# Graph attention in two layers: strip 0 of the next graph placed inside the previous graph's last sum

## Chip, cores and metric

One core of a Trainium2 chip. The core has five engines with an instruction queue each: TensorE (PE; its weight loads are a row of their own, PEld), VectorE (DVE), ScalarE (ACT), GpSimd (POOL) and SyncE (SP, which here issues most DMAs). The metric is the device time of one execution in microseconds; less is better. All times of the document are microseconds (us) unless they say ns.

## What is computed

16 graphs of 1024 nodes with 256 features, and a symmetric 0/1 adjacency with ones on its diagonal. Each graph passes through two attention layers, with a residual and a layer norm after each. The inputs give layer 0 one kind of edge only (`adj == 1`), so the reference comes down to this:

```
# layer 0, for one graph: x is 1024 x 256
e     = leaky_relu((x * a0) @ x.T, 0.2)
alpha = where(adj == 1, sigmoid(e), 0)
x     = layernorm(x + alpha @ x + bias)
# layer 1
H  = x @ W
s  = H @ a[:256];  d = H @ a[256:]
w  = where(adj != 0, exp(-leaky_relu(s[:, None] + d[None, :], 0.2)), 0)
h  = (w @ H) / w.sum(-1)
x  = layernorm(x + elu(h))
```

## The kernel before

The nodes of a graph are cut into 8 tiles of 128. For layer 0 the kernel computes only the upper triangle of the scores: strip `jt` holds rows of tile `jt` against the columns of tiles `jt` to 7. The lower triangle is the mirror image of it.

A strip goes through four steps, all written out by hand in program order (the schedule is manual; each engine takes its own instructions in that order, and waits on semaphores where it needs another engine's or a DMA's result):

- `strip` (L240): PE multiplies (L254) into one or two PSUM tiles of the pool `ps_e`, which has three. ACT takes Tanh twice, into `tb` (L262) and `low` (L263), and DVE takes the maximum (L264).
- `finish` (L270): DVE multiplies the strip with the adjacency into the tile `al`, which has one buffer.
- `dump` (L290, L294): DVE transposes `tb` in 32 x 32 blocks, and SP writes it to DRAM in four DMAs, so that DRAM holds the strip's mirror image `mir`. `tb` has four buffers.
- `gather` (L298): SP fetches the mirror image back, one DMA, into the column of `al` below the diagonal; `mask` (L305) then multiplies it with the adjacency on DVE. `add_twice` (L284) adds 2 on the diagonal, on POOL.

SP issues its DMAs in program order, and each of them uses one of eight semaphores in turn, so that a DMA can also have to wait for an earlier one's landing.

The loop over graphs `b` is a pipeline over three of them. An iteration does layer 0 of graph `b`, layer 1 of graph `prev = b - 1` and the output of graph `done = b - 2`:

- The strips of `b` (loop over `jt`, L783). After strip `jt` the list `projects` names the tiles of layer 1 of `prev` that are projected there: `project` (L582) multiplies `yT` with `W` into a PSUM tile of the pool `ps_acc`, which has three. ACT takes three small exponentials and scalings of it (L592 to L594) and evicts it as `H` (L603). The eviction of one projection is issued with the next projection. Also in this loop: dumps, gathers (`gather(b, jt - 1)` after dump `jt`, so fetch 0 stands behind dump 1), the deviations of the last two tiles of `done` (L344, ACT), and, from `jt` 4 on, the masks and the sums of blocks of `al` (`combine_al`, L455) that the seven products need.
- The seven block products of `alpha @ x` (L477: tiles `pQ`, `pV`, `pW`, `pR`), in Strassen's manner, evicted to `yT` and written to DRAM in row order (`turn_y`) and read back as rows `x1` (`fetch_y`). Product 1 (`pQ`) and product 5 (`pV`) stand between strips 4 and 7. `weights` (L637) makes layer 1's weights of `prev` on DVE.
- The sum of layer 1 of `prev` (L642), tile by tile. Tiles 0 to 2 run side by side, tiles 3 to 7 one after the other. The loop over `t` (L903) also holds the work behind each tile's sum: `elu` (DVE inverts the row sum, L678 and L679; ACT takes Relu and Exp, L687 and L688), `add` (DVE, L693 and L695), `deviation1` of the tile before and `deviation0` of graph `b` (ACT, L344), `roots0` on POOL, which gives the scalings `rcol` that the projections of `b` need, and `combine_x` for `b + 1`.

The adjacency of `b + 1` is loaded in two halves by POOL: rows of tiles 0 to 3 once `fetch_y` has landed (L888), rows of tiles 4 to 7 at tile 5 of the sum (L923). The PSUM pools of the sum's tiles are given by the string "aaeettat": tiles 2 and 3 take from `ps_e`, tiles 0, 1 and 6 from `ps_acc`, tiles 4, 5 and 7 from `ps_t`.

Of the kernel before, what the change touches and what calls it, by code (L numbers as in the profile page):

```python
# [30 lines left out]
def one_kind_pass(  # L31
# [35 lines left out]
    NT = N // P  # L67
# [172 lines left out]
    def strip(b, jt):  # L240


        if jt == 0:
            als[b] = one.tile([P, NT, N], F32, tag="al", name=f"al_{b}")
        width = N - jt * P
        tb = four.tile([P, N], F32, tag="tb", name=f"tb_{b}_{jt}")
        tbs[b, jt] = tb
        n_chunks = -(-width // HALF)
        per = -(-(width // P) // n_chunks) * P
        for n, o in enumerate(range(0, width, per)):  # L250
            w = min(per, width - o)
            pe = ps_e.tile([P, HALF], F32, tag="e", name=f"pe_{b}_{jt}_{n}")
            for c in range(ND):
                nc.tensor.matmul(  # L254
                    pe[:, 0:w],
                    lhsT=xTs[b][:, c, ts(jt, P)],
                    rhs=xas[b][:, c, ds(jt * P + o, w)],
                    start=(c == 0),
                    stop=(c == ND - 1),
                )  # L260
            low = two.tile([P, HALF], F32, tag="low", name=f"low_{b}_{jt}_{n}")
            nc.scalar.activation(tb[:, ds(o, w)], pe[:, 0:w], AF.Tanh, scale=0.5)  # L262
            nc.scalar.activation(low[:, 0:w], pe[:, 0:w], AF.Tanh, scale=0.5 * SLOPE)  # L263
            nc.vector.tensor_tensor(tb[:, ds(o, w)], tb[:, ds(o, w)], low[:, 0:w], ALU.max)  # L264
# [31 lines left out]
    def gather(b, t):  # L296

        nc.sync.dma_start(  # L298
            als[b][:, t + 1 :, ts(t, P)], mirs[b, t].rearrange("(jt p) i -> p jt i", p=P)
        )  # L300
# [406 lines left out]
    def deviation1(b, t):  # L707
        deviation(ys[b][t], mv1s[b][:, t, :])
# [66 lines left out]
    for b in range(1, B):  # L775
        prev, done = b - 1, b - 2
        last = b == B - 1

        projects = [[0, 1], [2], [3], [4, 5], [6, 7], [], [], []]
        if prev == 0:  # L780

            projects = [[], [], [0, 1], [2, 3], [4, 5, 6, 7], [], [], []]
        for jt in range(NT):  # L783
            if jt == 4:
                mask(b, 0, 0, HT)
                combine_al(b, 1, 0, 2)
            if jt == 5:
                new_yT(b)
                product(b, 1)
                mask(b, 1, 0, HT)  # L790
                save_p(prev, 0, NT, nc.scalar)
                share_p(prev, 0, NT)
                combine_al(b, 1, 2, 3)
                mask(b, 0, HT)
                mask(b, 1, HT)
                mask(b, 2, 0, HT)
                combine_al(b, 1, 3, HT)
                mask(b, 2, HT)
                if done >= 0:
                    r1s[done] = center(mv1s[done], f"1_{done}", unit=1.0 / D)  # L800
            if jt == 6:
                unite(b, "p1")
                product(b, 5)
                unite(b, "p5")
                combine_al(b, 2, 0, HT)
            strip(b, jt)
            if jt == 5:
                mask(b, 3, HT)
            finish(b, jt, ends=False)
            if jt == 4:  # L810
                gather(b, 3)
            if jt < NT - 1:
                dump(b, jt)
            if jt < 2 and done >= 0:
                deviation1(done, NT - 2 + jt)
            if prev == 0 and jt == 0:
                turn_x1(0, 0)
            if prev == 0 and jt == 1:
                transpose_x1(0)
            if jt >= 1 and jt != 4:  # L820
                gather(b, jt - 1)
            if jt < 4 and b == 1:
                combine_x(b, jt)
            for t in projects[jt]:
                project(prev, t)
            if jt == 4:
                evict_H()
            add_twice(b, jt)
        if not last:
            new_xT(b + 1)  # L830
            load_blocks(xTs[b + 1], x[b + 1], 0, N)

        def extras(n):
            if prev == 0 and n < 2:
                scale0(0, HT + 2 * n)
                scale0(0, HT + 2 * n + 1)
            elif prev > 0:
                scale0(prev, 2 * n)
                scale0(prev, 2 * n + 1)
            if done >= 0:  # L840
                for q in (2 * n, 2 * n + 1):
                    scale1(done, q)
                    if q == 3:
                        store(done, 0, HT)
            if n < 3:
                check_adj(b, n)

        product(b, 3)
        combine_al(b, 3, 0, HT)
        extras(0)  # L850
        product(b, 6)
        weights(prev, 0)
        mask(b, 4)
        mask(b, 5)
        combine_al(b, 4, 0, 2)
        mask(b, 6)
        combine_al(b, 4, 2, HT)
        unite(b, "u2")
        extras(1)
        product(b, 7)  # L860
        extras(2)
        product(b, 2)
        extras(3)
        unite(b, "s")
        unite(b, "c12")
        unite(b, "c22")
        unite(b, "c11")
        product(b, 4)
        turn_y(b, 0)
        if done >= 0:  # L870
            store(done, HT, HT)
        weights(prev, 1)
        weights(prev, 2)
        weights(prev, 3)
        weights(prev, 4)
        unite(b, "c21")
        turn_y(b, 1)
        fetch_y(b, 0)
        fetch_y(b, 1)
        if not last:  # L880
            load_x(b + 1, [nc.sync])
        check_adj(b, 3)
        weights(prev, 5)
        weights(prev, 6)
        weights(prev, 7)
        check_pq(prev)
        if not last:
            load_adj(b + 1, 0, behind=x1s[b][:, HT, 0:1])  # L888

        def sum_of(t):  # L890
            homes = {"a": (ps_acc, "acc"), "e": (ps_e, "e"), "t": (ps_t, "t")}
            return acc1(prev, t, *homes[("aaeteeaa" if last else "aaeettat")[t]])

        n_first = 3
        first = [sum_of(t) for t in range(n_first)]
        for m in range(NT):
            for t in range(n_first):
                sum1(prev, t, first[t], m)
        if not last:
            turn_x(b + 1, 0, False)  # L900
            turn_x(b + 1, 1, False)
        rinvs = invert_sums(prev, first)
        for t in range(NT):  # L903
            if t >= n_first:
                acc = sum_of(t)
                for m in range(NT):
                    sum1(prev, t, acc, m)
            if last and t == 7:
                for m in range(4):
                    weights(b, m, 0, HT)  # L910
            elu(prev, t, *((first[t], rinvs[t]) if t < n_first else (acc,)))
            if last and t in (2, 3):
                for q in range(HT):
                    stats0(b, (t - 2) * HT + q)
                roots0(b, t - 2)
            if t >= 1:
                add(prev, t - 1)
            if t >= 2:
                deviation1(prev, t - 2)
            if not last and t in (3, 5):  # L920
                sums0(b, (t - 3) // 2)
                if t == 5:
                    load_adj(b + 1, 1, behind=mv0s[b][:, HT, 0:1])  # L923
            if not last and t >= 4:
                for q in range(2 * t - 8, 2 * t - 6):
                    deviation0(b, q)
                if t % 2 == 1:
                    roots0(b, (t - 5) // 2)
            for n in ([0], [1], [2, 3])[t - 5] if not last and t >= 5 else []:
                combine_x(b + 1, n)  # L930
            if t == 3 and not last:
                scale_x(b + 1, 0)
                scale_x(b + 1, 1)
            if last and t in (4, 6):
                t0 = (t - 4) // 2 * HT
                for n in range(HT):
                    project(b, t0 + n)
                evict_H()
                save_p(b, t0, HT, nc.gpsimd)
                share_p(b, t0, HT)  # L940
            if last and t in (5, 7):
                for q in range(HT):
                    scale0(b, (t - 5) // 2 * HT + q)
            if last and t == 7:
                for m in range(4, 6):
                    weights(b, m, 0, HT)
        if not last:
            add(prev, NT - 1)
# [522 lines left out]
```

## Time and profile before

| what | value |
|---|---|
| median of 3 runs | 1219.75 us |
| lowest, highest | 1218.95, 1220.93 us |
| the profiled execution | 1221.67 us |
| its span, first to last instruction | 1219.9 us |
| granted TensorE clock in it | 0.998 |
| busy: PE matmul | 1208.1 us (99%), 4385 passes |
| busy: PE weight load | 820.6 us (67%) |
| busy: DVE | 993.7 us (81%) |
| busy: ACT | 842.8 us (69%) |
| busy: POOL | 385.5 us (32%) |
| SP's DMA queue | 136.90 MB, 56.5% of 16 engines' span |
| POOL's DMA queue | 41.95 MB, 18.6% |

A float32 matmul runs as two passes, each with its own weight load, so a count of passes is twice that of instructions. In a row of the timeline, the numbers are the start and the time taken, in us; then the engine, the line of the code, the operation, output and input by name, the sizes and how many were merged; in square brackets, how long the engine stood idle before it and what ended that. "SPq" rows are DMA issues. A row of the table by stretches gives a stretch, its length, the busy time of PE, PEld, DVE, ACT and POOL with the number of instructions, the granted clock, the mean busy share of the 16 DMA engines and the GB/s that they moved. A busy share says how long an engine had an instruction at work; whether another could have begun sooner is read from the starts.

### The profile page before, as it was taken

Reading aid. Unit: us, or ns where it says so; the run is one execution under the profiler, and the core shown is the slowest. Engines: PE = TensorE matmul, PEld = TensorE weight load, DVE = VectorE, ACT = ScalarE, POOL = GpSimd, SP = SyncE. Lnnn points to the kernel's source line nnn. Section 1 sums busy time; section 2 is a strip of 40 time slices with the busy share of each in tenths; the row PEclk is TensorE's granted clock in tenths of the full one; section 3 lists DMA queues with packets and bytes.
Section 4 is the critical chain, followed back from the end, with each engine's and each line's share of the span. In section 5 each row is a group of like instructions: output and inputs, shape, how many; then the busy total and the mean of one; then the engine's idle time right before and its main releaser. Section 6 shows DMA issues by size and latency. Waiting matters only on the chain.

```text
span 1219.9 us, 15900 instructions
## 1 busy us (share of the span) xinstructions
PE 1208.1 (99%) x4385; PEld 820.6 (67%) x4385; DVE 993.7 (81%) x1774; ACT 842.8 (69%) x2135; POOL 385.5 (32%) x715
## 2 busy tenths in 40 slices
PE   9999999999999999999999999999999999999997
PEld 7766758576575766758667485675857657576686
DVE  5698797887979879797897978979788896887966
ACT  3574866678677676876768766786676867667674
POOL 2220332414334043431424324143340433303343
PEclk9999999999999999999999999999999999999999
DMA  9568787697877968788787986978769787797412
GB/s 194 104 131 149 122 151 173 132 182 137 155 155 152 193 124 152 155 153 182 148 154 142 164 180 132 169 143 151 170 138 189 130 156 153 152 188 135 108 52 72
DMA packets 605080, 180.66 MB, mean 148 GB/s; under 512 B 482612, under 2 KB 587448, under 8 KB 604984
## 3 DMA queue, kind: packets, MB, share of 16 engines
q1 hardware_dynamic: 582800, 136.90, 56.5%
q0 software_dynamic: 20528, 41.95, 18.6%
q10 hardware_dynamic: 1656, 0.72, 0.2%
q8 instruction: 37, 0.61, 0.2%
q14 instruction: 59, 0.48, 0.1%
HBM read 152.44 MB, written 60.62 MB: 175 GB/s over the span
## 4 chain that ended last, share of the span: by engine, by line
PE 95%; DMA 2%; DVE 1%; ACT 1%; SPq 0%; issue 0%; ACTq 0%; DVEq 0%
PE acc L642 36%; PE pe L254 19%; PE pW L477 8%; PE pH L582 8%; PE pV L477 8%; PE pQ L477 8%; PE pR L477 4%; PE acc L396 2%; DMA al<-mir 1%; SPq L294 0%; DMA mir<-tb 0%; DMA x<-in_x 0%; PE pal L313 0%; PE pxT L230 0%; DVE al L270 0%
## 5 line engine op out<-in xcount | busy, mean ns | idle before, releaser
L642 PE MATMUL acc<-H,e 128*128 128x257 f32 x2032 | 444.8, 380 | 0.0
L642 PEld LDWEIGHTS acc<-H,e 128*128 128x128 f32 x2032 | 384.8, 190 | 63.4 <-issue 7.2
L254 PE MATMUL pe<-xa,xT 128*128 128x384 f32 (+1 forms) x720 | 250.0, 487 | 0.0
L254 PEld LDWEIGHTS pe<-xa,xT 128*128 128x128 f32 x720 | 134.4, 190 | 91.7 <-issue 52.9
L284 POOL TENSOR_TENSOR al<-ident,al 128x128 f32<-128x128 f32 x128 | 111.5, 879 | 201.7 <-DVE al L270 201.6
L637 DVE SCALAR_TENSOR_TENSOR e<-p,pq_kept,adj 128x1024 f32<-128x1024 f32 (+1 forms) x136 | 159.9, 1229 | 0.2 <-DMA p<-p_row 0.2
L262 ACT ACTIVATE tb<-pe 128x512 f32<-128x512 f32 (+1 forms) x192 | 93.8, 489 | 90.8 <-PE pe L254 63.9
L455 DVE TENSOR_TENSOR al<-al 128x1024 f32<-128x1024 f32 (+2 forms) x105 | 143.7, 1369 | 5.1
L264 DVE TENSOR_TENSOR tb<-tb,low 128x512 f32<-128x512 f32 (+1 forms) x192 | 104.2, 548 | 41.1 <-ACT low L263 41.0
L130 ACT ACTIVATE junk<-adj,minus 128x2048 bf16<-128x2048 bf16 x64 | 127.4, 1990 | 0.0
L582 PE MATMUL pH<-Wx,yT 128*128 128x258 f32 x480 | 116.4, 380 | 0.0
L104 POOL CAST adj<-x 128x1 bf16<-128x1 f32 x15 | 2.8, 187 | 348.7 <-DMA x<-y_rows 273.8
L582 PEld LDWEIGHTS pH<-Wx,yT 128*128 128x128 f32 x480 | 91.2, 190 | 31.1 <-issue 13.4
L477 PE MATMUL pV<-al,S 128*128 128x512 f32 x240 | 109.4, 595 | 0.9 <-DVE al L455 0.9
L305 DVE SCALAR_TENSOR_TENSOR al<-al,adj 128x512 f32<-128x512 f32 (+3 forms) x150 | 83.1, 570 | 30.9 <-DMA al<-mir 30.9
L477 PE MATMUL pW<-al,x 128*128 128x512 f32 x240 | 107.9, 592 | 0.0
L477 PE MATMUL pQ<-al,x 128*128 128x512 f32 x240 | 107.9, 592 | 0.0
L270 DVE SCALAR_TENSOR_TENSOR al<-tb,adj 128x512 f32<-128x512 f32 (+7 forms) x132 | 97.4, 738 | 4.5
L263 ACT ACTIVATE low<-pe 128x512 f32<-128x512 f32 (+1 forms) x192 | 94.0, 489 | 1.2 <-DVE tb L264 1.2
L668 ACT ACTIVATE sums<-acc,tiny 128x1 f32<-128x1 f32 x45 | 11.8, 262 | 118.2 <-PE acc L642 118.2
L379 ACT ACTIVATE y_kept<-y_kept,mr,r 128x256 f32<-128x256 f32 x120 | 64.9, 589 | 34.3 <-POOL mr L374 33.2
L477 PEld LDWEIGHTS pW<-al,x 128*128 128x128 f32 x240 | 45.5, 190 | 57.5 <-issue 55.3
(147 smaller groups left out, 1631.9 us busy)
## 6 DMA issues: line engine op xcount, KB each, us to landing
adj<-in_adjT POOLq DMA_DIRECT2D x30, 1024.0 KB, 8.3
x<-in_x SPq DMA_DIRECT2D x15, 1024.0 KB
y_rows<-Z SPq DMA_DIRECT2D x240, 64.0 KB
x<-y_rows SPq DMA_DIRECT2D x30, 512.0 KB
out<-y_kept SPq DMA_DIRECT2D x30, 512.0 KB
xT<-in_x SPq DMA_DIRECT2D x112, 128.0 KB
p<-p_row POOLq DMA_DIRECT2D x15, 512.0 KB, 4.1
mir<-tb SPq DMA_DIRECT2D x60, 112.0 KB
```

What stands on the lines that cost most here:

```text
L130: nc.scalar.activation(junk, rows, AF.Square, bias=minus1, scale=2.0, accum_out=chk[:, b * CHECKS + n : b * CHECKS + n + 1],)
L254: nc.tensor.matmul(pe[:, 0:w], lhsT=xTs[b][:, c, ts(jt, P)], rhs=xas[b][:, c, ds(jt * P + o, w)], start=(c == 0), stop=(c == ND - 1),)
L262: nc.scalar.activation(tb[:, ds(o, w)], pe[:, 0:w], AF.Tanh, scale=0.5)
L263: nc.scalar.activation(low[:, 0:w], pe[:, 0:w], AF.Tanh, scale=0.5 * SLOPE)
L264: nc.vector.tensor_tensor(tb[:, ds(o, w)], tb[:, ds(o, w)], low[:, 0:w], ALU.max)
L270: nc.vector.scalar_tensor_tensor(als[b][:, jt, c0:c1], tbs[b, jt][:, c0 - jt * P : c1 - jt * P], 1.0, adjs[b, jt // HT][:, jt % HT, c0:c1] ...
L284: nc.gpsimd.tensor_tensor(diag, ident2, diag, ALU.add)
L455: nc.vector.tensor_tensor(out_, in0, in1, ALU.subtract)
L477: nc.tensor.matmul(banks[bank], lhsT=lhs[:, jt, :], rhs=rhs[:, jt, :], start=first and jt == 0, stop=jt == HT - 1, skip_group_check=True,)
L582: nc.tensor.matmul(pt, lhsT=x1Ts[b][:, c, ts(t, P)], rhs=Wx[:, c, :], start=(c == 0), stop=(c == ND - 1),)
L637: nc.vector.scalar_tensor_tensor(e, p_bcs[b][:, cols], q, rows, ALU.mult, ALU.min)
L642: nc.tensor.matmul(acc, lhsT=es[b][:, m, ts(t, P)], rhs=Hs[b][m], start=(m == 0), stop=(m == NT - 1),)
```

## The change

Three edits, for graphs 2 to 15 (graph 1 keeps its order):

- Strip 0 of graph `b + 1` with its product with the adjacency and its dump is issued in the sum of layer 1 of `prev`, ahead of tile 6. So that tile 5's `add` and tile 4's `deviation1` do not stand behind it, they are moved up in front of it.
- In the next iteration the loop over strips leaves those steps out at `jt` 0 and issues the fetch of mirror 0 there, ahead of strip 1 and dump 1 instead of behind dump 1.
- The projections stand behind strips 1, 2, 3 and 4, two to a strip, where they stood behind strips 0 to 4 as 2, 1, 1, 2, 2.

```diff
-        projects = [[0, 1], [2], [3], [4, 5], [6, 7], [], [], []]
+        projects = [[], [0, 1], [2, 3], [4, 5], [6, 7], [], [], []]
...
-            strip(b, jt)
+            ahead = jt == 0 and b > 1
+            if not ahead:
+                strip(b, jt)
             if jt == 5:
                 mask(b, 3, HT)
-            finish(b, jt, ends=False)
+            if not ahead:
+                finish(b, jt, ends=False)
             if jt == 4:
                 gather(b, 3)
-            if jt < NT - 1:
+            if jt < NT - 1 and not ahead:
                 dump(b, jt)
...
+            if ahead:
+                gather(b, 0)
-            if jt >= 1 and jt != 4:
+            if jt >= (1 if b == 1 else 2) and jt != 4:
                 gather(b, jt - 1)
...
         for t in range(NT):
+            if t == 6 and not last:
+                add(prev, t - 1)
+                deviation1(prev, t - 2)
+                strip(b + 1, 0)
+                finish(b + 1, 0, ends=False)
+                dump(b + 1, 0)
             if t >= n_first:
                 acc = sum_of(t)
...
-            if t >= 1:
+            if t >= 1 and (last or t != 6):
                 add(prev, t - 1)
-            if t >= 2:
+            if t >= 2 and (last or t != 6):
                 deviation1(prev, t - 2)
```

The instructions are the same in kind and number on every engine; only their order changes.

## The prediction, made before the changed kernel had run

> **What bounds the kernel now.** The page first: TensorE (PE) is busy for nearly the whole span and makes up nearly the whole chain that ended last.
>
> ```profile
> PE   9999999999999999999999999999999999999997
> ...
> PE 95%; DMA 2%; DVE 1%; ACT 1%; SPq 0%; issue 0%; ACTq 0%; DVEq 0%
> ```
>
> As the ends of matmuls are modelled, I took their starts. Successive matmul passes begin 0.216 us apart at 257 columns, 0.322 at 384 and 0.429 at 512, in every stage and every graph. All passes at these spacings add up to 1197.6 us; from the first to the last start there are 11.9 us more. 9.2 of these lie in the start-up, in graph 1 (one wait for an evicted accumulator, 0.8 us) and in the last graphs' tail, which the change leaves alone. The other 2.7 us are seven gaps. Six of them are one place, the product V of a graph, which waits for `combine_al`, which waits for a mirrored strip. Graph 2, timeline of PE, DVE and SP:
>
> ```profile
> 154.65 1.02 PE L477 MATMUL pQ<-al,x 128*128 128x512 f32 x2
> 156.80 2.74 PE L477 MATMUL pV<-al,S 128*128 128x512 f32 x6
> 160.05 1.12 PE L477 MATMUL pV<-al,S 128*128 128x512 f32 x2 [0.51 <-DVE al L455]
> ```
>
> ```profile
> 158.90 0.29 DVE L305 SCALAR_TENSOR_TENSOR al<-al,adj 128x128 f32<-128x128 f32 x1 [1.25 <-DMA al<-mir]
> 159.30 0.69 DVE L455 TENSOR_TENSOR al<-al 128x512 f32<-128x512 f32 x1
> ```
>
> ```profile
> 140.62 5.73 SPq L294 DMA_DIRECT2D mir<-tb  x8
> 146.52 0.45 SPq L298 DMA_DIRECT2D al<-mir  x1
> 147.41 3.03 SPq L294 DMA_DIRECT2D mir<-tb  x4
> 150.55 0.45 SPq L298 DMA_DIRECT2D al<-mir  x1
> 151.04 4.49 SPq L294 DMA_DIRECT2D mir<-tb  x4
> 155.69 1.75 SPq L298 DMA_DIRECT2D al<-mir  x2
> ```
>
> Six passes from 156.80 make the seventh due at 156.80 + 6 x 0.429 = 159.37; it begins at 160.05, 0.68 late, and the pair lasts 1.12 where the pair of product Q lasts 1.02: 0.78 us in all. DVE waited 1.25 us for the fetch of mirror 2. On SP's queue that fetch is the first of the last row. The gaps at V: 0.78, 0.68, 0.28, 0.20, 0.23, 0.27 us (graphs 2, 3, 4, 10, 11, 15), sum 2.44; the seventh, 0.26, is a late weight of layer 1 in graph 3. So 2.7 us is what any change here can win.
>
> **The change, part by part.** Times below are counted from the first matmul of tile 5 of layer 1's sum (272.10 us in the span for graph 4), where both orders still agree.
>
> PE: the same matmuls in another order, and the third projection (`pH` of tile 3) is due at 22.08 in both, in all 14 graphs. Cost 0 while no operand is late.
>
> Mirrors. In graph 4 dump 0 is issued at 18.8, fetch 0 at 25.0, dump 2 at 25.6, fetch 1 at 29.4. Dump 2 stands behind fetch 0, which lands at 29.6: its four issues take 3.6 us and its first part lands at 30.1, where dump 1, with no fetch ahead of it, takes 2.1 to 2.6 us in the graphs. Fetch 1 follows dump 2, lands at 33.2; the last part of dump 3 waits for that landing (they share a semaphore), and fetch 2 stands behind it, at 33.6. After the change fetch 0 goes out when dump 0 has landed, about 17.2 (below), and lands about 21.4, ahead of dump 1 at 22.4. Dump 2 begins 0.2 later (below), 25.8, is issued in dump 1's 2.1, so fetch 1 goes out at 28.1, 1.3 earlier. It lands 1.7 behind the last landing of dump 2 (as before), 30.0 + 1.7 = 31.7, 1.5 earlier, and fetch 2 with it. The largest gap at V is 0.78: all six close, with 0.6 us or more to spare, and DVE reaches the weights earlier too, so the seventh closes. Gain 2.7; bounds 0 (rival B) and 2.7.
>
> ACT and DVE, the price of it. Rows of graph 4 around strip 0:
>
> ```profile
> 287.11 0.60 ACT L263 ACTIVATE low<-pe 128x512 f32<-128x512 f32 x1
> 287.59 0.52 ACT L344 ACTIVATE dev_junk<-y_kept,mv 128x256 bf16<-128x256 f32 x1
> ...
> 288.08 0.28 ACT L592 ACTIVATE H<-pH,rcol 128x1 f32<-128x1 f32 x1
> ...
> 289.37 0.46 ACT L603 ACTIVATE H<-pH,wr 128x256 f32<-128x256 f32 x1
> ```
>
> ```profile
> 287.75 0.69 DVE L264 TENSOR_TENSOR tb<-tb,low 128x512 f32<-128x512 f32 x1 [0.28 <-ACT low L263]
> 288.53 1.23 DVE L270 SCALAR_TENSOR_TENSOR al<-tb,adj 128x1024 f32<-128x1024 f32 x1
> 289.79 1.11 DVE L290 STREAM_TRANSPOSE tb<-tb 128x896 f32<-128x896 f32 x1
> ```
>
> I walk the new order with the spacings of these rows. ACT ends tile 5's two deviations as before, then deviation of tile 4 at 6.76 and the four Tanh at 7.26, 7.74, 8.22, 8.69. DVE: second maximum 0.64 behind the last Tanh, 9.33; product with the adjacency 0.78 later, 10.11; transpose 1.26 later, 11.37; only behind it (1.03) the inverse sum of tile 6, 12.41. ACT's `elu(6)` waits for that: 12.86, after 3.7 us with nothing to do. From there ACT never waits: two evictions 0.37 + 0.36, deviations 0.63 + 0.51, `elu(7)` 0.37 + 0.36, four deviations 0.63 x 3 + 0.51, four Tanh of strip 1 0.48 + 0.48 + 0.39 + 0.37, a deviation 0.49, then the projections' seven small ones 1.28: the eviction of the first projection (L603) begins at 21.34 and ends at 21.80. PE needs it for `pH` 3, the fourth project in a ring of three accumulators, at 22.08: 0.28 ahead.
>
> What a shorter lead costs: three places of the trace show it. Where the releaser ended 0.094 us after the matmul was due, PE lost 0.150 + 0.106; 0.521 after, 0.577 + 0.104; 0.039 before (graph 1's `pH`), 0.015 + 0.105. So the loss is 0.16 minus the lead. With 0.28 it is 0, and 0.12 is left over; the links' spread in the 14 graphs is 0.01 to 0.02 each. Between 0 and 0.16 x 14 = 2.2 us (lead gone) I take 0. ACT is then 0.5 behind the old order at strip 2, whose transpose ends 0.2 later (25.81 for 25.61); at projects 4 to 7 it has caught up.
>
> The adjacency. Strip 0's finish now comes at 10.1 instead of 16.4, and needs the half of the next adjacency whose load is issued about -1. It lands at 6.6 to 9.0 in 13 graphs and at 10.5 in graph 7. Cost there 0.4 - 0.12 = 0.3 us; elsewhere 1.1 us or more of cover. If all loads were as late, 14 x 0.3 = 4 us; I take 0.3.
>
> DMA. The mean share of the DMA engines in stretches of 3 us, graph 4:
>
> ```profile
> 284.00:287.00 3.00, 3.00 (x10) 1.69 (x10) 2.08 (x6) 2.93 (x10) 1.62 (x3) 1.00 0.87 165
> 287.00:290.00 3.00, 3.00 (x11) 1.74 (x10) 2.60 (x4) 2.94 (x12) 2.59 (x6) 1.00 0.00 0
> ...
> 299.00:302.00 3.00, 3.00 (x12) 1.87 (x11) 1.32 (x3) 2.54 (x9) 0.46 (x1) 1.00 1.01 212
> ```
>
> Dump 0's four writes and fetch 0 leave the full stretch at 299 (1.01) for 284.6 to 293, of which 3 us stood empty. They meet the tail of the other adjacency half (lands 15.1, needed at 31): if both ran at half speed there, dump 0 lands 2.5 later and fetch 0 at 24, needed at 28.6. No cost. On SP nothing stands behind dump 0 and fetch 0 until dump 1; the fetch's wait for dump 0's landing (4.6 us after issue) ends at 17.2. POOL's second set of `roots0` starts 3.7 us later with deviation (17.4) and ends about 22.4; project 4 needs it at 26.6. Cost 0.
>
> Sum: 1221.67 us for the profiled execution (span 1219.9 and 1.8 around it) - 2.7 + 0.3 = 1219.3. That execution is 1.9 above the median of the runs, 1219.75. If the 1.9 is all late mirrors, the median run has 0.8 of them to lose: 1219.3. If none of it is: 1217.4. I take the middle, **1218.4**, own range 1217.2 to 1219.6.
>
> [...]
>
> **Rivals.**
> A, slower: ACT's walk is later than I make it, at `elu(6)` behind DVE's finish and transpose, and `pH` 3 waits in every graph. For it: ACT is busy 2.9 of 3 us there (the 284 and 287 rows), and only 0.12 us is to spare. Against: every link is a row. It decides from 0.12 us; the gain of 1.35 in the median is used up at 0.12 + 1.35/14 = 0.22 us. At 0.4: 1218.4 + 14 x 0.28 = 1222.3.
> B: dump 2's slow issues are not fetch 0's doing. Then its 0.2 us later start makes each of the six gaps 0.2 larger and opens some 0.15 in two graphs with little lead: 1219.75 + 1.5 + 0.3 = 1221.5.
> C, faster beyond the measure: the profiled execution's extra time is fixed, and the runs have all 2.7 us of gaps or more: 1217.0.
> D: PE has room that starts don't show. The idle of the strips' weight loads is 57.0 us in 238 waits, 0.24 each; strip 0's four in 14 graphs would give 13.4: 1206.
>
> **How the numbers follow.** Forecast 0.44, A 0.25, B 0.14, C 0.14, D 0.02, none of these 0.01. What a measurement of this kernel tells from no change is about 0.2%, 2.4 us: faster is below 1217.3 (C, D and a little of the forecast), slower above 1222.2 (most of A, a little of B). Faster 0.17, within 0.58, slower 0.25. Range 1216.9 to 1222.6, which leaves out D and the late end of A.
>
> **What would show it.** V's last pair 1.02 us long in all graphs, and DVE's L305 no longer idle for mirror 2; fetch 0 issued near 17 and dump 2's four issues in 2.1 us; ACT idle 3.7 us ahead of `elu(6)`; `pH` 3 at 22.08. Wrong: a gap of PE at `pH` 3 in every graph (A), gaps at V still there (B), DVE waiting at L270 for `adj` in more than one or two graphs.

## The result and the profile after

The changed kernel's median is 1216.93 us (1215.74 to 1218.59, 13 runs); the kernel before, run beside it, has 1219.75 (1218.89 to 1222.18, 13 runs). The ratio is 0.9975, 95% interval 0.9967 to 0.9984: 2.8 us faster, where 1.35 was forecast. The profiled execution took 1216.93, with a span of 1215.1 and a granted clock of 0.998.

The page of after, busy shares of PE in 40 slices and the chain of work that ended last:

```profile
PE   9999999999999999999999999999999999999997
...
PE 90%; DVE 3%; DMA 2%; ACT 2%; issue 1%; SPq 1%; POOL 0%; ACTq 0%; DVEq 0%; POOLq 0%
```

PE is as full as before. The chain has 3% of DVE and 2% of ACT, because it is followed back through one place where PE did wait (graph 11's `pH`, below).

Product V of graph 2, timeline of PE and of DVE:

```profile
154.51 3.60 PE L477 MATMUL pV<-al,S 128*128 128x512 f32 x8
157.95 1.25 PE L254 MATMUL pe<-xa,xT 128*128 128x256 f32 x6
```

```profile
155.11 0.29 DVE L305 SCALAR_TENSOR_TENSOR al<-al,adj 128x128 f32<-128x128 f32 x1 [0.99 <-DMA al<-mir]
155.50 0.69 DVE L455 TENSOR_TENSOR al<-al 128x512 f32<-128x512 f32 x1
```

The eight passes are one row now: from 154.51 to 157.95 they take 3.44 = 8 x 0.43, with no gap. DVE still waits for mirror 2, 0.99 us, but its `combine_al` ends at 156.19, and the seventh pass is due at 154.51 + 6 x 0.429 = 157.08. A wait is there, and it costs nothing. SP's queue in the same graph:

```profile
132.01 2.85 SPq L294 DMA_DIRECT2D mir<-tb  x4
137.35 0.38 SPq L298 DMA_DIRECT2D al<-mir  x1
141.88 5.62 SPq L294 DMA_DIRECT2D mir<-tb  x8
147.66 0.41 SPq L298 DMA_DIRECT2D al<-mir  x1
148.14 3.54 SPq L294 DMA_DIRECT2D mir<-tb  x4
151.85 1.74 SPq L298 DMA_DIRECT2D al<-mir  x2
```

Fetch 0 (137.35) is alone between dump 0 and dump 1; the next row is dumps 1 and 2 in one, and fetch 1 follows at 147.66. Over all graphs DVE waited for mirrors 30.9 us before and 11.7 after, by the list of waits (total, times, longest), first of before, then of after:

```profile
DVE al L305 <- DMA al<-mir: 30.9, 31, 1.6
```

```profile
DVE al L305 <- DMA al<-mir: 11.7, 15, 1.4
```

Strip 0 in graph 4, DVE and then ACT. From tile 5's first matmul (268.10 here) the product with the adjacency begins at 10.12, `elu(6)` at 12.83, and the eviction of the first projection ends at 21.74:

```profile
278.22 1.23 DVE L270 SCALAR_TENSOR_TENSOR al<-tb,adj 128x1024 f32<-128x1024 f32 x1
279.48 1.11 DVE L290 STREAM_TRANSPOSE tb<-tb 128x896 f32<-128x896 f32 x1
```

```profile
280.93 0.47 ACT L687 ACTIVATE h<-acc,rinv 128x256 f32<-128x256 f32 x1 [3.52 <-DVE rinv L679]
...
289.38 0.46 ACT L603 ACTIVATE H<-pH,wr 128x256 f32<-128x256 f32 x1
```

What is new on PE's path is `pH` of tile 3 in a few graphs. Graph 11, PE, DVE and ACT:

```profile
810.00 1.03 PE L582 MATMUL pH<-Wx,yT 128*128 128x258 f32 x4
811.48 1.14 PE L582 MATMUL pH<-Wx,yT 128*128 128x258 f32 x4 [0.44 <-ACT H L603]
```

```profile
799.79 1.24 DVE L270 SCALAR_TENSOR_TENSOR al<-tb,adj 128x1024 f32<-128x1024 f32 x1 [1.02 <-POOL mr L373]
```

```profile
802.51 0.47 ACT L687 ACTIVATE h<-acc,rinv 128x256 f32<-128x256 f32 x1 [4.47 <-DVE rinv L679]
...
810.96 0.46 ACT L603 ACTIVATE H<-pH,wr 128x256 f32<-128x256 f32 x1
```

Four passes of 0.217 from 810.00 make the fifth due at 810.87; it begins at 811.48, 0.61 late. Followed back: the eviction came 0.94 late, because `elu(6)` did, because DVE's product with the adjacency began 11.05 after tile 5's first matmul instead of 10.12. The bracket names POOL, but nothing in that product needs POOL's `mr`; by the DMA's own times the adjacency's half landed at 10.92, issued at 0.34 where other graphs have -2.3 to -0.4. The bracket names whatever ended last before the start.

The mean share of the DMA engines in graph 4, where the empty stretch was, and where fetch 1 and dump 3 run:

```profile
280.00:283.00 3.00, 3.00 (x13) 2.25 (x12) 2.19 (x8) 2.04 (x7) 0.86 (x5) 1.00 1.15 205
283.00:286.00 3.00, 3.00 (x11) 1.88 (x11) 2.29 (x7) 2.90 (x11) 0.47 (x2) 1.00 0.73 111
...
295.00:298.00 3.00, 3.00 (x12) 1.87 (x11) 2.83 (x5) 2.75 (x10) 0.45 (x1) 1.00 0.80 131
```

The stretch of 283 to 286 stands for 287 to 290 of before, which was empty; it now carries dump 0's tail and fetch 0.

**Where the time went.** I cut each profiled execution in three: the start (first matmul to graph 1's first `pH`), the steady stretch (from there to the last matmul), and the end (start of the last matmul to the end of the span). The gaps at V are the sum of what its spacings exceed 0.429 us; those at `pH` leave graph 1 out. Before and after were profiled three times each (the further two of each are among the experiments):

| us | before, three profiles | after, three profiles |
|---|---|---|
| start | 65.1, 63.4, 62.9 | 62.8, 62.8, 63.5 |
| steady stretch | 1144.42, 1144.25, 1144.15 | 1142.99, 1142.42, 1141.83 |
| of it gaps at V | 2.44, 2.52, 2.31 | 0, 0.26, 0 |
| of it gaps at `pH` | 0, 0, 0 | 1.20, 0.44, 0.10 |
| end | 9.35, 9.56, 9.27 | 8.32, 8.15, 8.26 |

On the means the steady stretch lost 1144.27 - 1142.41 = 1.86 us: 2.33 less at V, 0.58 more at `pH`, and the late weight of graph 3, which only the first profile of before has. The end lost 9.39 - 8.24 = 1.15. Together 3.0, where the runs show 2.8. The start varies by 2 us from execution to execution, whichever kernel runs.

### The profile page after: what moved, and what is told of

Its sections match the earlier page's. It is cut to its first block, busy times and chain, and to the rows that moved or that the text cites. A ratio compares the mean times of both kernels' runs of the same rounds, so it can differ in the third digit from the quotient of the medians.

```text
span 1215.1 us, 15998 instructions
## 1 busy us (share of the span) xinstructions
PE 1205.0 (99%) x4385; PEld 819.4 (67%) x4385; DVE 1003.9 (83%) x1774; ACT 834.3 (69%) x2135; POOL 387.1 (32%) x715
## 4 chain that ended last, share of the span: by engine, by line
PE 90%; DVE 3%; DMA 2%; ACT 2%; issue 1%; SPq 1%; POOL 0%; ACTq 0%; DVEq 0%; POOLq 0%
PE acc L642 33%; PE pe L254 18%; PE pH L582 8%; PE pV L477 8%; PE pQ L477 8%; PE pW L477 8%; PE pR L477 4%; PE acc L396 2%; DMA adj<-in_adjT 1%; DMA al<-mir 1%; DVE al L455 1%; DVE e L637 1%; ACT dev_junk L344 0%; DMA x<-y_rows 0%; DVE al L270 0%
## 5 line engine op out<-in xcount | busy, mean ns | idle before, releaser
L264 DVE TENSOR_TENSOR tb<-tb,low 128x512 f32<-128x512 f32 (+1 forms) x192 | 112.6, 594 | 62.0 <-ACT low L263 60.1
L284 POOL TENSOR_TENSOR al<-ident,al 128x128 f32<-128x128 f32 x128 | 108.9, 864 | 143.1 <-DVE al L270 143.0
L687 ACT ACTIVATE h<-acc,rinv 128x256 f32<-128x256 f32 x81 | 38.2, 471 | 89.1 <-DVE rinv L679 78.1
L305 DVE SCALAR_TENSOR_TENSOR al<-al,adj 128x512 f32<-128x512 f32 (+3 forms) x150 | 82.5, 566 | 11.7 <-DMA al<-mir 11.7
```

The costliest lines, as they stand in the source:

```text
L284: nc.gpsimd.tensor_tensor(diag, ident2, diag, ALU.add)
```

## Experiments

Times in this section are medians, each beside runs of the kernel before on the same chip (1219.6 to 1220.0).

**The changed kernel again, and the kernel before twice more.**

> The changed kernel once more, for a second profile. Theory (the gain is the closed gaps at product V, and the runs of the kernel before hold at least the 2.7 us of them that its profile shows): again 0.997 to 0.998 of the kernel before, V's last pair 1.02 us in all 14 graphs, all passes' excess at 512 columns under 0.4 us; gaps at pH 3 of 0.1 to 0.6 us in two to four graphs, not the same ones (late adjacency), 0.5 to 1.5 us in all. Rival (the profile of after had luck in its start and its drain, 1.8 and 1.0 us shorter than in before's profile): the median is back at 0.999 or more.

> The changed kernel, as the measure for the other three: 1216.4 to 1217, steady 1142.4 to 1143, gaps at pH 3 in two to four graphs, 0.3 to 1.2 us in all.

> The kernel before once more, for a second profile. From the first matmul of graph 1's pH to the last matmul of the program it took 1144.4 us in the first profile, with 2.6 us of gaps at V; the start ahead of that took 65.1 us (after, twice: 62.8) and the time behind the last matmul 9.4 (after, twice: 8.3 and 8.1). Theory (the runs of before hold more of V's gaps than its profile shows, and that profile's extra time was in the start and the drain): V's gaps sum to 3 us or more, the steady stretch takes 1144.8 to 1146, the start about 63 to 64 us, the drain about 8.3. Rival (the gaps are the profile's, and the kernel before always starts and drains slower): steady 1144.4 or less, start 65, drain 9.4 again.

> The same, a third profile of the kernel before: V's gaps 3 us or more by the theory, 2.6 or less by the rival; start 63 to 65 us, and drain 8.3 by the theory, 65 and 9.4 by the rival.

Measured: after 1216.42 (ratio 0.9971, 0.996 to 0.9982) and 1216.79 (0.9975, 0.9966 to 0.9984); the profiled executions of before 1220.05 and 1219.13. Their parts are in the table above. What was expected of `a_again` holds: the ratio, V closed but for 0.26 us, and gaps at `pH` in two graphs, if with 0.44 us a little smaller than expected. `after_c` has less at `pH` (0.10 in one graph) than the 0.3 to 1.2 us expected, and a shorter steady stretch. Of before's theory and rival, neither holds as written. The runs of before do not hold more than 2.7 us of gaps: V has 2.3 to 2.5 in every execution. Of the rival, half is right: the slow start was chance (63.4 and 62.9 the next times), but the longer end was there each time. In the second profile of after the late adjacency is named where it was hidden in the first, graph 11 again:

```profile
799.27 1.23 DVE L270 SCALAR_TENSOR_TENSOR al<-tb,adj 128x1024 f32<-128x1024 f32 x1 [0.60 <-DMA adj<-in_adjT]
```

**The end of the program.** Up to the last output's DMA issue, 4.6 us behind the last matmul, both kernels do the same at the same times. Then ACT, between its last semaphore event and its last drain, takes 1.3 to 1.6 us in before and 0.1 in after. To test whether this hangs on the length of ACT's program, two kernels got tiny copies in a place where ACT is idle. The edit of the first kernel (of before; the second, of after, has 9 and 7 copies for 2):

```diff
     nc.vector.memset(minus1, -1.0)
+    pad = const.tile([P, 1], F32, tag="pad", name="pad")
...
+        for _ in range(2 if b >= 2 else 0):
+            nc.scalar.copy(pad, minus1)
         if not last:
             load_adj(b + 1, 0, behind=x1s[b][:, HT, 0:1])
```

> The kernel before with 28 tiny instructions more on ACT, copies of one column, two in each of graphs 2 to 15, in a place where ACT stands idle for 7 us. So its ACT program has the length that the changed kernel's has (2599 records instead of 2571). In the trace, all four executions in before's ACT program end 9.2 to 9.6 us behind the last matmul, all six in the changed one's 8.1 to 8.4; the difference lies between ACT's last semaphore event and its last drain (1.3 to 1.6 us against 0.1). Theory (what ends later is the load of the last piece of ACT's program, which falls on another place when the program is 28 instructions longer; so 1.1 to 1.2 us of the gain have nothing to do with strips, mirrors or projections): the end comes 8.1 to 8.4 behind the last matmul, the stretch from graph 1's pH to the last matmul stays at 1144.1 to 1144.5; time 1.1 less than before, about 1218.6, ratio 0.999. Rival (the drain is shorter because of the order in which the last graph's work ends): 9.2 to 9.6 us again, ratio 1.000.

> The other way round: the changed kernel with 100 tiny copies more on ACT in that idle place (7 in each graph, 9 in graph 2). [...] Theory: the end comes 9.2 to 9.6 us behind the last matmul, the rest as in after (1142.4 to 1143.0): 1.1 us more than after, about 1217.8, ratio 0.9985. Rival (no matter of place): 8.1 to 8.4, ratio 0.9973.

Measured: before with 28 copies 1218.51 (0.9988, 0.9979 to 0.9997), after with 100 copies 1217.84 (0.9983, 0.9974 to 0.9992): within 0.1 of what the theory said, both times. As the intervals reach about 1 us to either side, agreement that close is partly luck; the ends in the traces show the effect more sharply. ACT's last records and the end of the span, in us behind the start of the last matmul:

```
kernel                     ACT records  last event  last drain  end of span
before                     2571         7.68        8.99        9.35
after                      2599         7.66        7.75        8.32
before + 28 copies         2599         7.63        7.72        8.29
after + 100 copies         2699         7.57        8.83        9.18
projections put back       2585         7.57        7.66        8.23
projections alone          2571         7.54        8.96        9.32
```

The length of ACT's program decides it, not the work: 28 instructions more take the wait away from the old order, 100 more bring it into the new one. The other engines' programs do not decide it: with fetch 0 put back (below) SP's program has the length of before and PE's that of after, with fetch 0 alone it is the other way round, and the end goes by ACT's in both, as in all 18 profiled executions: 8.1 to 8.5 us behind the last matmul with 2585 and 2599 records, 9.2 to 9.6 with 2571 and 2699. The 28 instructions that the change adds to ACT only wait for a semaphore (366 in its program before, 394 after); SP has 28 more of them, too, and PE 42 more. So what the section on the change says, that the instructions are the same in kind and number, holds for the computing instructions and the DMAs alone. The steady stretches (1144.31 and 1142.51) are those of before and after.

What ACT waits for there is not shown; that it is a load of its program, as the theory has it, no run shows. In the kernels with the wait, and in no other, one more 8 KB packet of an instruction queue starts 9.5 to 9.9 us behind the last matmul (9.66 in the first profile of before). That is 0.65 us or more behind the start of ACT's last drain (8.99 there), and behind the end of the span (9.35), so it cannot be what the drain waited for; what it belongs to is not shown either. What is shown is that programs 128 instructions apart (2571 and 2699 records) end alike; a period that divides 128 would do the same. Both end 11 records behind a multiple of 128, and those without the wait (2585 and 2599) end 25 and 39 behind one. With the 28 semaphore waits and the 100 copies ACT's program is 128 longer than in before; why that brings the wait back, and whether there is a period at all, no run shows.

**Fetch 0 put back behind dump 1**, nothing else:

```diff
-            if ahead:
-                gather(b, 0)
-            if jt >= (1 if b == 1 else 2) and jt != 4:
+            if jt >= 1 and jt != 4:
                 gather(b, jt - 1)
```

> The change without its last part: fetch 0 goes out behind dump 1 again, where it stood before, and only that is put back. Theory (fetch 0 ahead of dump 2 on SP's queue is what made dump 2's issues slow and fetches 1 and 2 late): dump 2's first to fourth issue takes 1.9 to 2.6 us again instead of 1.46, fetch 1 goes out at 29 to 29.6 instead of 28.17 (from tile 5's first matmul), gaps at V come back in at least the six graphs of the kernel before and about 0.2 us larger each, as dump 2 begins 0.2 later; the late adjacency's 0.5 to 1.2 us at pH 3 stay. Sum: before + 1.2 + 0.3 to 1.2, about 1221.3 to 1222, ratio 1.001 to 1.002. Rival 1 (the gain is the relief of ACT and DVE by strip 0 and the projections being moved, whatever fetch 0 does): V stays closed and the ratio at 0.9975. Rival 2 (fetch 0 is early enough by dump 0's move alone, since dump 0 has landed long before and the fetch waits for nothing): between, 0.998 to 0.9995, with half of the gaps.

> The kernel with fetch 0 behind dump 1 once more, for a second profile: its first one was an execution of 1218.37 where its median is 1219.44, and its gaps at V summed to 1.9 us in two large and one small place. Theory (without the early fetch V's gaps are there again, in places that change from run to run): V's gaps 2 to 4 us, the last matmul to the end 8.1 to 8.4. Rival (they come back only by chance in a graph or two): under 1.5 us.

> Fetch 0 behind dump 1 again, timed once more on the same chip as the changed kernel. If the timing is right: 1219 to 1219.8, 2.4 to 3.2 above the changed kernel, and this profile's steady stretch (graph 1's pH to the last matmul) 1144.5 to 1145.2, with 2.5 to 3.5 us of gaps at V. If the two profiles are right: 1218 to 1218.5, 1.2 to 1.8 above, steady 1143.6 to 1144.

Measured: 1219.44 (0.9995, 0.9986 to 1.0003) and, at the second timing, 1218.42 (0.9988, 0.9979 to 0.9997). In three profiles the gaps at V are 1.85, 1.48 and 1.93 us, at `pH` 0.32, 0.11 and 0.44, the steady stretch 1143.95, 1143.58 and 1144.09. Graph 10 of the third, PE, DVE and SP:

```profile
750.94 2.74 PE L477 MATMUL pV<-al,S 128*128 128x512 f32 x6
754.12 1.12 PE L477 MATMUL pV<-al,S 128*128 128x512 f32 x2 [0.45 <-DVE al L455]
```

```profile
752.98 0.29 DVE L305 SCALAR_TENSOR_TENSOR al<-al,adj 128x128 f32<-128x128 f32 x1 [1.09 <-DMA al<-mir]
```

```profile
741.91 3.62 SPq L294 DMA_DIRECT2D mir<-tb  x4
745.64 0.46 SPq L298 DMA_DIRECT2D al<-mir  x1
746.14 3.62 SPq L294 DMA_DIRECT2D mir<-tb  x4
749.93 1.72 SPq L298 DMA_DIRECT2D al<-mir  x2
```

It is the picture of before: fetch 0 (745.64) between dump 1 and dump 2, fetch 1 at 749.93, and the pair of V's passes late. So fetch 0 ahead of dump 1 is worth 1.5 us of the steady stretch. What fetch 0 does to dump 2 shows in dump 2's four issues, graph 4, first of before, then of after:

```profile
297.73 3.63 SPq L294 DMA_DIRECT2D mir<-tb  x4
```

```profile
294.12 1.99 SPq L294 DMA_DIRECT2D mir<-tb  x4
```

In the mean over the graphs the four take 3.1 to 3.2 us in the three profiles of before, 2.6 to 2.8 with fetch 0 put back, and 2.0 to 2.1 in after. The fourth issue alone takes 0.75 to 2.0 us in every graph of the six profiles with fetch 0 right ahead of dump 2, and 0.5 to 0.63 in every graph of after's three. The rest of the difference, 0.4 to 0.5 us, is gone without moving fetch 0; dump 2 begins 0.4 later there than in before, and whether that is the cause is not shown.

The theory's time, 1221.3 to 1222, was missed by some 2 to 3 us. It had V's gaps larger than in before, and they are 0.7 smaller; its sum also started from before's longer end, where this kernel has after's (8.4 to 8.5). With most of the gaps and a ratio of 0.9988 to 0.9995, the number is near rival 2's. Fetch 1 leaves at 28.9 in the mean, as in before, so that the gaps are no larger is understood; why they are smaller is not. The first timing lies 1.0 above the second, and above what the profiles can explain; the second agrees with them (after 1216.79, 1.6 less). The intervals of the two ratios overlap, so this may be chance.

**Fetch 0 alone**, in the order of before, so that it stands ahead of dump 1 but dump 0 is where it was:

```diff
+            if jt == 0 and b > 1:
+                gather(b, 0)
-            if jt >= 1 and jt != 4:
+            if jt >= (1 if b == 1 else 2) and jt != 4:
                 gather(b, jt - 1)
```

> The kernel before, with strip 0 and the projections left where they were, and only fetch 0 put ahead of dump 1 on SP's queue. Theory (fetch 0 is only worth moving because dump 0 has been moved ahead of it): fetch 0 waits for dump 0's landing at 23.5, dump 1, due at 22.45, stands behind it and goes out 1.1 to 1.5 us late and in slow issues, and all that follows in the queue with it: fetch 1 no earlier than 28.7, dumps 2 and 3 later; V's gaps at least as large as before in most graphs, 0.2 to 0.6 us each: 1222 to 1226, ratio 1.002 to 1.005. Rival (any order in which fetch 0 doesn't stand ahead of dump 2 is enough, and strip 0 needn't have moved): dump 2 in 1.5 us, V closed, 1217, ratio 0.9975.

Measured: 1237.19 (1.0137, 1.0122 to 1.0153). Graph 2, SP and PE:

```profile
143.22 0.38 SPq L298 DMA_DIRECT2D al<-mir  x1
143.69 5.98 SPq L294 DMA_DIRECT2D mir<-tb  x8
149.87 0.38 SPq L298 DMA_DIRECT2D al<-mir  x1
```

```profile
154.66 2.74 PE L477 MATMUL pV<-al,S 128*128 128x512 f32 x6
158.58 1.12 PE L477 MATMUL pV<-al,S 128*128 128x512 f32 x2 [1.18 <-DVE al L455]
```

The seventh pass is 158.58 - (154.66 + 6 x 0.429) = 1.35 late. The mechanism is the theory's, its size far larger: SP stands at fetch 0 until dump 0 has landed (23.5 to 24.3 from tile 5's first matmul), dump 1 goes out at 24.0 to 24.7, dump 2 at 27.4 to 28.3, fetch 1 at 29.9 to 31.3. In the mean over the graphs fetch 1 is 1.3 us later than in before (30.2 for 28.9), and V loses 18.7 us, 16.3 more: 1.2 a graph. Some 2 us more are lost at strips of graphs 9 and 10. In before V had next to no slack, so the delay of fetch 1 counts nearly in full in each of 14 graphs; the expectation had 0.2 to 0.6.

**The projections.** First after with the old list, then before with the new list:

```diff
-        projects = [[], [0, 1], [2, 3], [4, 5], [6, 7], [], [], []]
+        projects = [[0, 1], [2], [3], [4, 5], [6, 7], [], [], []]
```

> The changed kernel with the projections where they were (two ahead of strip 1, one each behind strips 1 and 2), so only strip 0 and fetch 0 are moved. Theory (the projections were moved only to balance ACT's work, and what is left at pH 3 is a late adjacency against a lead of 0.3 us): pH 3 then comes earlier in the queue but its accumulators are free long before, no gap there in graphs with a late adjacency; V closed; time within 0.1% of after, ratio 0.9965 to 0.998. Rival (with projections 0 and 1 directly behind layer 1's sum, PE needs evictions from ACT while ACT still has tile 7's elu and deviations to do): a new gap at pH 2 or at strip 1 in every graph, 0.1 to 0.5 us each, 1.4 to 7 us in all: ratio 0.9985 to 1.003.

> The kernel before with the projections alone moved behind strips 1 to 4, strip 0 and fetch 0 left. Theory (where the projections stand decides when dump 1 and dump 2 go out: in the changed kernel with the old places dump 1 went out at 24.13 instead of 22.39, dump 2 at 26.92 instead of 26.02): here strip 1 comes ahead of projections 0 and 1, dump 1 goes out earlier than 22.45, fetch 0 with it or right behind, dump 2 no earlier than 25.6; V's gaps 1 to 3 us, steady 1143 to 1145; ACT's program has the old length or another, so the end is 8.1 to 8.4 or 9.2 to 9.6. Rival (with strip 0 still ahead of strip 1 and no projection between them, PE waits for an accumulator or ACT at strip 1 in every graph): 0.2 to 1 us each, ratio 1.002 to 1.012.

Measured: 1219.53 (1.000, 0.9991 to 1.0009) and 1218.17 (0.9987, 0.9978 to 0.9997). SP's queue of after with the old list, graph 4:

```profile
281.55 2.85 SPq L294 DMA_DIRECT2D mir<-tb  x4
287.81 0.38 SPq L298 DMA_DIRECT2D al<-mir  x1
293.16 4.79 SPq L294 DMA_DIRECT2D mir<-tb  x8
298.12 0.41 SPq L298 DMA_DIRECT2D al<-mir  x1
```

Fetch 0 is early, but with projections 0 and 1 ahead of strip 1 dump 1 goes out at 24.13 from tile 5's first matmul (after: 22.39), dump 2 at 26.92 (26.02), fetch 1 at 29.09 (28.17), and V's gaps are back: 2.06 us, steady 1144.45. I had taken the new places of the projections for a matter of ACT's load; they are what brings strip 1, and so dumps 1 and 2, forward. The rival's gap at `pH` 2 or strip 1 in every graph did not show; only graph 11, whose adjacency was late (10.80), lost 0.66 at a strip, so a late adjacency is not free here either. By the parts of its profile this kernel should lie 1 us below before (the end is 8.23, the steady stretch is before's); its timing puts it 0.2 below, within the interval. The projections alone do not help: dump 2 begins up to 0.6 earlier, but its issues behind fetch 0 take 2.2 to 2.9, fetch 1 leaves at 28.5 to 29.3, V loses 2.32, steady 1144.10. By its steady stretch and end this kernel differs from before by 0.2 us, by its timing by 1.7 (0.4 to 2.7 by the interval); that difference stays open. Differences of a microsecond between medians are not safe here without the parts of a trace beside them.

**The late `pH` 3.** Strip 0's product with the adjacency, transpose and dump behind `elu(6)`; the adjacency's load let go one landing earlier; and both:

```diff
                 strip(b + 1, 0)
-                finish(b + 1, 0, ends=False)
-                dump(b + 1, 0)
...
             elu(prev, t, *((first[t], rinvs[t]) if t < n_first else (acc,)))
+            if t == 6 and not last:
+                finish(b + 1, 0, ends=False)
+                dump(b + 1, 0)
```

```diff
-            load_adj(b + 1, 0, behind=x1s[b][:, HT, 0:1])
+            load_adj(b + 1, 0, behind=x1s[b][:, 0, 0:1])
```

> The change with strip 0's product with the adjacency, its transpose and its dump behind elu(6) instead of ahead of it. Theory (pH 3 is late only because DVE waits for the adjacency and elu(6) stands behind that): finish 0 comes at 11 to 12.5 instead of 10.12, so the loads that land at 10.5 to 10.9 are in time and elu(6) waits for none; no gap at pH 3; dump 0 about 1.5 to 2 us later, fetch 0 out by 20 and landed by 24, V still closed. Time: after's 1216.9 less 0.9 to 1.2, about 1215.9, ratio 0.9965. Rival (elu(6) earlier only moves the wait: the finish, then ahead of other DVE work, makes strip 1's maximum or elu(7) late): pH 3's lead goes in every graph, 0.1 to 0.3 each, 1.4 to 4 us more than after, ratio 0.9987 or above.

> The changed kernel, with the load of the next adjacency's first half held back until the first half of the other operand's fetch has landed, not the second. Theory (what is left at pH 3 is the adjacency landing at 10.4 to 10.9, and it lands so because it is issued late): the load goes out 0.5 to 1.5 us earlier in each graph, lands before 10 in all 14, no gap at pH 3: after less 0.8 to 1.2 us, ratio 0.9965. Rival (landing is set by what the DMA engines carry at that time, not by the issue): lands no earlier, or the fetch it then runs beside lands later and holds the x transposes; ratio 0.9975 or above.

> The changed kernel with strip 0's finish, transpose and dump behind elu(6), and the adjacency's load let go one landing earlier: the two edits that each took away the late pH 3. Theory (after them PE waits for nothing in a graph but what was there before: graph 1's pH, the start, the tail): from graph 1's pH to the last matmul 1141.6 to 1142 us (after 1143.0 and 1142.4), 0.7 to 1.2 less than after; median 1215.9 to 1216.3, ratio 0.9965 to 0.997. Rival (either edit alone had taken all there was, and a later dump 0 costs it again at V in some runs): 1216.5 to 1217, ratio 0.9973 to 0.9978, no better than after.

> Strip 0's finish behind elu(6) and the adjacency's load let go earlier, once more, beside the changed kernel. If the late pH 3 (0.4 and 1.2 us in two profiles of the changed kernel) is really gone from every execution: steady 1141.7 to 1142, median 0.4 to 1 below the changed kernel's. If it is replaced by something the profiles do not show: the same median within 0.2.

Measured: 1216.75 (0.9972, 0.9963 to 0.9982), 1216.49 (0.9975, 0.9964 to 0.9985), both 1216.36 (0.9972, 0.9962 to 0.9983) and 1216.64 (0.9971, 0.996 to 0.9982). Graph 11 with the product behind `elu(6)`, DVE:

```profile
801.31 0.16 DVE L678 TENSOR_SCALAR rinv<-acc 128x1 f32<-128x1 f32 x1 [0.57 <-PE acc L642]
801.51 0.17 DVE L679 RECIPROCAL rinv<-rinv 128x1 f32<-128x1 f32 x1
801.59 1.23 DVE L270 SCALAR_TENSOR_TENSOR al<-tb,adj 128x1024 f32<-128x1024 f32 x1
```

The inverse sum of tile 6 comes first, then the product, which begins at 10.87 in all 14 graphs; the adjacency that landed at 10.23 here was in time. The gap at `pH` 3 is gone from every graph, steady 1141.72. With the earlier load the adjacency lands by 8.0 everywhere, and only graph 9's 0.1 is left (its product begins 0.28 late in every profile of after, of fetch 0 put back and of the earlier load, with the adjacency there, but not with the old list of projections; the cause is open), steady 1142.07. So both edits do to the trace what the theory said, and the medians do not show it: 0.2 us or less from after. In the second profile of both edits one slow landing of fetch 1 (33.43, where most are 31.2 to 32.1) cost 0.8 at V, and in the tail PE waited 0.66 longer for an eviction of `H` (L603) than elsewhere, steady 1143.24. Chance of that size may hide what the edits win, which these runs do not settle. No version here is measurably faster than the changed kernel.

## Why the prediction was right or wrong

- *PE is full, what can be won are gaps at V.* Right. V's gaps are 2.3 to 2.5 us in every profile of before, 0 to 0.26 after. Of the 9.2 us that the prediction puts down to the start-up, graph 1 and the tail, some 3.3 are no gaps at all: the 257- and 258-column passes begin 0.217 to 0.218 us apart in the mean, and it summed them with 0.216. The sum does not rest on that. PE had no room that starts don't show (rival D, 1206 us): the spacings stayed at 0.217 (257 columns) and 0.429.
- *Mirrors.* Right in each time, within 0.7 us in graph 4: fetch 0 out at 17.9 (forecast 17.2; up to 20.6 in graph 11, still ahead of dump 1) and landed at 21.8 (21.4), dump 2 at 26.02 (25.8), fetch 1 at 28.17 (28.1), landed at 31.4 to 31.9 (31.7). That DVE would not wait for mirror 2 at all was wrong; it waits 1 us, ahead of its due time. Rival B, that dump 2's slow issues were not fetch 0's doing, falls: the four issues take 2.0 us with fetch 0 away (forecast 2.1) and 2.6 to 2.8 with it put back, and fetch 1 leaves 0.6 later.
- *ACT's walk.* `elu(6)` forecast at 12.86, measured 12.83; the eviction's end 21.80, measured 21.74; `pH` 3 at 22.08. Rival A falls: no gap in 11 to 13 of 14 graphs. The rule "0.16 minus the lead" held: graph 7 had a lead of -0.23 and lost 0.39, graph 9 had 0.06 and lost 0.10.
- *The adjacency.* Right in kind, too small: 0.3 us in one graph was forecast from one profile's landings; three profiles have 1.20, 0.44 and 0.10, mean 0.58, in up to three graphs.
- *The sum.* Here it failed, at the step "I take the middle". The 1.9 us by which the profiled execution lay above the median were shared out as "all late mirrors" or "none"; halving gave a gain of 1.35. Two more profiles show that none of it was late mirrors: the gaps were the same 2.3 to 2.5, and the 1.9 lay in the start (65.1 against 62.9 and 63.4). By the forecast's own terms 2.7 - 0.3 = 2.4 should have stood; 1.9 was measured in the steady stretch.
- *The term that was missing.* "9.2 of these lie in the start-up, ... and in the last graphs' tail, which the change leaves alone" was right of the matmuls, but the end behind the last one was looked at in no step: the order of the tail's work is unchanged, but the program of ACT is 28 instructions longer, and its end comes 1.15 us sooner. The prediction put the end at nothing without a look at it. Two kernels that change that length alone show it, in both directions. Without it the changed kernel would stand at an estimated 1217.8 to 1218.1, by the kernel with 100 copies (1217.84) and by 1216.93 + 1.15: close to the forecast of 1218.4, whose halved gain had no ground.
- *Rival C* (1217.0) had the time, in part by luck. It was right that the profiled extra time was no late mirrors and that V's gaps were there to win in full (2.3 won). But the runs held no more gaps than the profile, 0.58 was lost at `pH`, and 1.15 came from the program's end, which it did not have.

## What to carry to other kernels

Before an execution's extra time is shared out, cut it into start, steady stretch and end, and compare with a second profile: here the steady stretch of one kernel agreed within 0.3 us (before) and 1.2 us (after, by its late adjacency), while starts differed by 2 us with no regard to the kernel. A reordering can also change how many instructions an engine's program has (here 28 more on ACT, and an end 1.15 us sooner); when a kernel differs by about 1 us more than its waits explain, look at what each engine does behind its last useful instruction. In a queue shared by dumps and fetches, a fetch that waits for a landing belongs where that landing is already past and nothing urgent stands behind it: here moving it forward alone cost 17 us, and moving its producer first made it worth 1.5 us of the steady stretch.

## What the runs showed of the hardware

- The end of the program took 1.15 us more or less by the length of ACT's program: 9.2 to 9.6 us behind the last matmul with 2571 and 2699 records, which are 128 apart, and 8.1 to 8.5 with 2585 and 2599.
- The start, up to graph 1's first `pH`, took 62.8 to 65.3 us in 18 profiled executions, independent of the kernel.
- DMA issues behind a fetch under way in the same queue were slower: dump 2's four issues took 2.0 to 2.1 us in 39 of 42 graphs of the changed kernel, where fetch 0 had landed, and 2.85 to 3.65 in the 42 graphs of before, where it stood right ahead of them.
